# Two of seven Strassen products of the first FFN matmul by a second level of the scheme

## Chip, core and metric

The kernel runs on one core of a Trainium2 chip. The metric is the device time of one launch in microseconds. A launch is measured several times; the median counts. One further execution is recorded by the hardware profiler, and all profile rows come from that one.

The engines are called PE (TensorE, matmul; PEld are its weight loads), DVE (VectorE), ACT (ScalarE), POOL (GpSimd) and SP (SyncE, which only issues DMAs here). SBUF is the memory on the core, PSUM the memory into which PE writes (eight banks).

## What is computed

The input `x` is [64 batch, 64 rows, 1024]. Two layers follow one another, and the result is added to `x`:

```python
# 1. a state-space convolution along the last axis, masked by the length of the row
kernel = 2 * einsum('hn,hnl->hl', Cs, exp(dtA * arange(L))).real
y = irfft(rfft(u * mask, 2 * L) * rfft(kernel, 2 * L))[..., :L] + u * mask * D
y = y * mask
# 2. a gated low-rank FFN: 64 experts of rank 16, the best 16 per token
scores = xf @ Wr.T                                   # xf = y as [4096, 1024]
G = softmax over the top 16 of 64 scores, 0 elsewhere
h = einsum('nd,krd->nkr', xf, A)                     # first FFN matmul:  1024 x 1024 per token
out = einsum('nkr,kdr->nd', h * G[:, :, None], B)    # second FFN matmul: 1024 x 1024 per token
return x + 2.0 * out
```

All in fp32.

## The kernel before

**Groups.** The 64 rows are handled in 8 groups of 8 rows, so a group has 512 tokens. For each group g the kernel builds tables of the convolution (`tables`, DVE and ACT), makes states and their recurrence (`into_states`, L742 and `recur`, L786), the convolution itself on PE (`inside`, L828 and L836, and `across`, L851), brings the result from PSUM to SBUF with the mask (`evict`, L862, tile `y`), computes gates (`gates`, L941 to 986, and `spread_gates`, which sends them through HBM and back into tiles `gx` by POOL DMAs at L1007), and runs the first FFN matmul (`first`, `seven`). After the eighth group the second FFN matmul runs over pairs of groups (`second`, L1272); it is not touched except for the place from which it loads its rows.

**The first FFN matmul.** It is a matrix of 1024 x 1024 (left side, `wa`) times 1024 x 512 (right side, the group's `y`), by one level of Strassen's scheme in Winograd's form: both sides are cut into 2 x 2 blocks, the left factors are summed once at the start, the right factors for each group by DVE (`right_factors`), and seven products of 512 x 512 by 512 x 256 remain in place of eight. The left factors are `a11, a12, s4, a22, s1, s2, a21` for products 1 to 7; the right factors are `b11, b21, b22, t4, t1, t2, b12`.

`seven` goes over the seven products twice, for `j` = 0 and 2: each time for half of the 512 output rows. One product of one half is `product(n)`, L681 to 695: eight matmul calls (two row blocks `ii`, four steps `k` of the contraction) of 128 x 128 weights with 256 moving columns (L687). The results go to a PSUM bank of the pool `ps_f`, which has four. The order within a half and what happens to each product are:

- product 1 into bank `c11`, copied by ACT to `p1` (L702)
- product 6; DVE: `u2 = p1 - p6` (L709)
- product 2 added into `c11`
- product 7; DVE: `u3 = p7 + u2` (L716)
- product 5 into bank `c12`; DVE: `c22 = -u3 - c12` (L720, shown as L503 by the profile, the line of the helper)
- product 4; DVE: `u3 = p4 - u3` (L1050, shown as L492)
- product 3 added into `c12`; then `finish`

**`finish`** (L1027) multiplies the four blocks by their gates: block 11 by DVE straight out of PSUM (L1041), the others by POOL (L1034), into a tile `hg` with room for seven blocks. `hg` has one buffer. The first three blocks are stored to `hg_dram` by a POOL DMA; later `sums` makes the four sums that the second matmul wants as right factors (DVE, L492) and stores four more blocks. `sums` is called by `sum_factors` after the second step of the following half.

**Interleaving.** `seven` is a generator with seven steps per half, 14 per group. The main loop pulls steps between the parts of the next group's convolution: the last five steps of group g-1's products and the first five of group g lie between two convolutions' parts, four steps between `inside(0, 1)` and `inside(2, 3)`. Within the engines' queues the instructions are ordered by a planner when the program is built, from its own cost estimates; a few are pinned to the order of the source (`keep_in_program_order`) or behind another instruction (`issue_after`). So an instruction can stand earlier on its engine than in the source. Each engine then works through its queue in that order.

**Start.** Before the first group the left factors are loaded and summed: `s1` and `s2` through PE with an identity matrix, `a21` and `s4` by accumulating POOL DMAs (`third_sum`, L230, and `fourth_sum`, L236 and L239).

**SBUF.** It is full. 16384 bytes per partition are held back for the descriptors of POOL's DMAs.

Of the kernel before, what the change touches and what calls it, by code (L numbers as in the profile page):

```python
# [37 lines left out]
F32 = mybir.dt.float32  # L38
I32 = mybir.dt.int32
AF = mybir.ActivationFunctionType  # L40
ALU = mybir.AluOpType
# [3 lines left out]
P = 128  # L45
NB = 64
NH = 64
L = 1024
# [12 lines left out]
HT = TOK // NS2  # L61
KH = NBLK // 2
# [45 lines left out]
def body(ctx: ExitStack, tc, x, xo, lens, par, dvec, dgrp, at, bm, wt, cst, out):  # L108
    nc = tc.nc
# [6 lines left out]
    def pool(stack, name, bufs, side, **kw):  # L116
        return stack.enter_context(tc.tile_pool(name=name, bufs=bufs, side=side, **kw))
# [9 lines left out]
    fp = pool(ctx, "fp", 2, "left")  # L127
    gp = pool(left, "gp", 1, "left")
    tq = pool(left, "tq", 1, "left")
    ids = pool(ctx, "ids", 1, "right")  # L130
    const = pool(right, "const", 1, "right")
    xp = pool(right, "xp", 4, "right")
# [99 lines left out]
    def fourth_sum(s4, s2):  # L232

        for k in range(0, KH, 2):
            tc.keep_in_program_order(
                G.dma_start(s4[:, k : k + 2, :], at[:, KH + k : KH + k + 2, : L // 2]))  # L236
        for k in range(0, KH, 2):
            tc.keep_in_program_order(
                G.dma_start(s4[:, k : k + 2, :], s2[:, k : k + 2, :], accum_op=ALU.add))  # L239
# [247 lines left out]
    def new(name, w=NP, dtype=F32, keep=False):  # L487
        pool = const if keep else prep
        return pool.tile([P, w], dtype, tag=f"p_{name}", name=f"p_{name}")

    def tt(o, a, b, o_):
        V.tensor_tensor(out=o, in0=a, in1=b, op=o_)  # L492
        return o
# [8 lines left out]
    def stt(o, a, s, o1, b, o2):  # L502
        V.scalar_tensor_tensor(out=o, in0=a, scalar=s, in1=b, op0=o1, op1=o2)  # L503
        return o
# [169 lines left out]
        tt(t4, b21, t2, ALU.subtract)  # L674
        return b11, b21, b22, t4, t1, t2, b12

    def seven(fac, rf, j, name, finish, second_early=False):

        def product(n, bank=None, more=False):  # L681
            first = bank is None
            if first:
                bank = ps_f.tile([P, 2, HT], F32, tag="pf", name=f"{name}_{j}_{n}")
            for ii in range(2):
                for k in range(KH):
                    nc.tensor.matmul(  # L687
                        bank[:, ii, :],
                        lhsT=fac[n - 1][:, k, (j + ii) * P : (j + ii + 1) * P],
                        rhs=rf[n - 1][:, k, :],  # L690
                        start=(first and ii == 0 and k == 0),
                        stop=(ii == 1 and k == KH - 1 and not more),
                        skip_group_check=True,
                    )
            return bank

        def new(t, n=0):
            return fp.tile([P, 2, HT], F32, tag=t, name=f"{name}_{j}_{t}{n}")

        c11 = product(1, more=True)  # L700
        p1 = new("p", 1)
        marks["p1"] = nc.scalar.copy(p1, c11)  # L702
        yield
        if second_early:
            product(2, c11)
            yield
        p6 = product(6)
        u2 = new("u2")
        marks["u"] = V.tensor_tensor(out=u2, in0=p1, in1=p6, op=ALU.subtract)  # L709
        yield  # L710
        if not second_early:
            product(2, c11)
            yield
        p7 = product(7)
        u3 = new("u3")
        marks["u"] = V.tensor_tensor(out=u3, in0=p7, in1=u2, op=ALU.add)  # L716
        yield
        c12 = product(5, more=True)
        c22 = new("p", 5)
        stt(c22, u3, -1.0, ALU.mult, c12, ALU.subtract)  # L720
        yield
        p4 = product(4)
        yield
        product(3, c12)
        finish(j, c11, u2, u3, c12, p4, c22)
        yield


    begun = {}
# [39 lines left out]
    def conv(g, steps, out):  # L769
# [102 lines left out]
        if g == 0:  # L872
            step(1)
            into_states(0, 0, bt, states, more)
            into_states(0, 1, bt, states, more)
            step(3)
            masks()
            first_order.close()
            step(1)
            behind_landing(toep[0:1, HG - 1, 0:1])  # L880
            third_sum(wa_quarters[0])
            fourth_sum(wa[2], wa[5])
            prep_ctx.close()
            fourth.append(pool(right, "sp_more", 1, "right"))
        recur(0, 1)
# [128 lines left out]

    hg_dram = dram.tile([NG, P, 7, KH, HT], F32, tag="hg", name="hg_dram")

    def first(g, y, spread):

        v = y.rearrange("p k s h b -> p k s (h b)")

        rf = [v[:, :KH, 0, :], v[:, KH:, 0, :]]
        if g:
            rf[:] = right_factors(v, f"ty{g}_")

        def finish(j, c11, u2, u3, c12, p4, c22):  # L1027
            hg = hp.tile([P, 7, 2, HT], F32, tag="hg", name=f"hg_{g}_{j}")

            def gate(m, s):  # L1030
                return spread[m, j][:, :, s * HT : (s + 1) * HT]

            def gt_(o, a, b, op):
                G.tensor_tensor(out=o, in0=a, in1=b, op=op)  # L1034

            def store(a, b):
                nc.gpsimd.dma_start(hg_dram[g, :, a:b, j : j + 2, :], hg[:, a:b])  # L1037

            b11, b21, b22, t4, t1, t2, b12 = (hg[:, n] for n in range(7))
            def first_quarter():  # L1040
                i = V.tensor_tensor(out=b11, in0=c11, in1=gate(0, 0), op=ALU.mult)  # L1041
                if late_gates:
                    tc.keep_in_program_order(i)


            late_gates = g in (0, NG - 1)
            if not late_gates:
                first_quarter()
            gt_(b22, c22, gate(1, 1), ALU.mult)
            tt(u3, p4, u3, ALU.subtract)  # L1050
            gt_(b21, u3, gate(1, 0), ALU.mult)
            marks["u"] = V.tensor_tensor(out=u2, in0=c12, in1=u2, op=ALU.add)
            gt_(b12, u2, gate(0, 1), ALU.mult)
            if late_gates:
                first_quarter()
            store(0, 3)

            def sums():
                tt(t1, b11, b12, ALU.subtract)
                tt(b12, b22, b12, ALU.subtract)  # L1060
                tt(t2, b22, t1, ALU.add)
                tt(t4, b21, t2, ALU.subtract)
                store(3, 7)

            unsummed.append(sums)

        for j in range(0, KH, 2):
            for n, _ in enumerate(seven(wa, rf, j, f"h{g}", finish, g + j == 0)):
                if n == 1:
                    sum_factors()  # L1070
                yield
                if n == 1 and len(rf) == 2:

                    rf[:] = right_factors(v, f"ty{g}_")

    unsummed = []

    def sum_factors():
        while unsummed:
            unsummed.pop()()  # L1080
# [13 lines left out]
    def queued(o, i):  # L1094
        tc.keep_in_program_order(nc.sync.dma_start(o, i))

    def load_factor(sg, n, halves):
        for gg in range(2):
            queued(halves[gg], hg_dram[2 * sg + gg, :, n - 1])

    def second_sums(r, u1, u2, u4, pinned=False):

# [409 lines left out]
```

## Time and profile before

| | |
|---|---|
| median of 3 runs | 942.14 us (941.78 to 942.18) |
| the profiled execution | 941.79 us |
| its span, first to last instruction | 940.0 us |
| granted PE clock | 1.00 throughout |
| busy: PE, PEld, DVE, ACT, POOL | 929.5, 743.2, 741.0, 164.1, 337.0 us |
| matmul records at L687 (first FFN matmul) | 1792 |
| the first 55 us | tables and convolution of the first group, sums of the left side |
| 55 to 597 us | eight groups of products with the next group's convolution in between |
| 597 to 940 us | the second FFN matmul |

A row of a group reads: line, engine, operation, output and inputs by tile name, shape, count | busy time in us, mean ns of one | idle time of the engine just before, and what ended it. A row of the chain or the timeline reads: start in us, length in us, engine, line, operation, count. A matmul's own length is longer than the distance to the next one, as they are pipelined; the distance is what a stream costs.

### The profile page before, as it was taken

Reading aid. Unit: us, or ns where it says so; the run is one execution under the profiler, and the core shown is the slowest. Engines: PE = TensorE matmul, PEld = TensorE weight load, DVE = VectorE, ACT = ScalarE, POOL = GpSimd, SP = SyncE. Lnnn points to the kernel's source line nnn. Section 1 sums busy time; section 2 is a strip of 40 time slices with the busy share of each in tenths; the row PEclk is TensorE's granted clock in tenths of the full one; section 3 lists DMA queues with packets and bytes.
Section 4 is the critical chain, followed back from the end, with each engine's and each line's share of the span. In section 5 each row is a group of like instructions: output and inputs, shape, how many; then the busy total and the mean of one; then the engine's idle time right before and its main releaser. Section 6 shows DMA issues by size and latency. Waiting matters only on the chain.

```text
span 940.0 us, 14255 instructions
## 1 busy us (share of the span) xinstructions
PE 929.5 (99%) x5384; PEld 743.2 (79%) x5384; DVE 741.0 (79%) x1725; ACT 164.1 (17%) x314; POOL 337.0 (36%) x284
## 2 busy tenths in 40 slices
PE   7999999999999999999999999999999999999998
PEld 2576768688588588588588788888888888888887
DVE  8899798797996995995892497879856866785674
ACT  5343233411411411510300000000000000000000
POOL 0113213052052052052052032356746555764555
PEclk9999999999999999999999999999999999999999
DMA  8635335347454444444242463754672574358332
GB/s 291 186 87 168 107 110 156 108 126 189 125 144 154 124 138 159 125 128 169 90 131 101 152 246 124 255 203 140 212 275 79 191 270 155 110 205 307 95 123 101
DMA packets 72298, 149.47 MB, mean 159 GB/s; under 512 B 10054, under 2 KB 21030, under 8 KB 72230
## 3 DMA queue, kind: packets, MB, share of 16 engines
q1 hardware_dynamic: 52546, 99.65, 32.1%
q0 software_dynamic: 16864, 47.22, 16.0%
q10 hardware_dynamic: 2820, 1.70, 0.6%
q8 instruction: 42, 0.69, 0.3%
q14 instruction: 26, 0.21, 0.1%
HBM read 100.13 MB, written 47.33 MB: 157 GB/s over the span
## 4 chain that ended last, share of the span: by engine, by line
PE 93%; DVE 6%; issue 0%; DMA 0%; ACT 0%; DVEq 0%
PE h L687 39%; PE s L1272 35%; PE pu L742 5%; PE pc L851 4%; PE psh L947 3%; PE pc L828 3%; PE pc L836 1%; DVE bt L492 1%; DVE hg L492 1%; DVE f L492 1%; DVE f L503 0%; PE psc L959 0%; PE pb L440 0%; PE last L1272 0%; DMA par_sb<-in_par 0%
## 5 line engine op out<-in xcount | busy, mean ns | idle before, releaser
L786 DVE SCALAR_TENSOR_TENSOR s<-s,turn 128x64 f32<-128x64 f32 (+1 forms) x432 | 122.8, 330 | 2.8 <-ACT s L747 2.3
L687 PE MATMUL h<-y,waa 128*128 128x256 f32 x512 | 116.7, 380 | 0.0
L687 PE MATMUL h<-y,was 128*128 128x256 f32 x512 | 116.2, 379 | 0.0
L687 PE MATMUL h<-ty,was 128*128 128x256 f32 x512 | 116.0, 379 | 0.0
L687 PEld LDWEIGHTS h<-y,waa 128*128 128x128 f32 x512 | 96.3, 190 | 15.0 <-issue 1.9
L687 PEld LDWEIGHTS h<-ty,was 128*128 128x128 f32 x512 | 97.1, 190 | 13.9 <-issue 0.8
L687 PEld LDWEIGHTS h<-y,was 128*128 128x128 f32 x512 | 96.8, 190 | 13.7 <-DVE b L503 0.4
L1034 POOL TENSOR_TENSOR hg<-h_p,gx 128x512 f32<-128x512 f32 x16 | 35.6, 2223 | 141.6 <-DVE h_p L503 107.1
L1007 POOL DMA_DIRECT2D gx<-gt_dram x56 | 33.9, 618 | 145.1 <-DMA gt_dram<-gt 145.1
L1286 ACT COPY p<-s 128x512 f32<-128x512 f32 x28 | 16.4, 585 | 312.4 <-PE s L1272 312.4
L1034 POOL TENSOR_TENSOR hg<-h_u,gx 128x512 f32<-128x512 f32 x32 | 45.1, 1409 | 63.8 <-DVE h_u L492 36.6
L1131 POOL TENSOR_TENSOR o<-o,acc_a 128x512 f32<-128x512 f32 x32 | 47.6, 1506 | 41.4 <-ACT acc_a L1149 32.5
L687 PE MATMUL h<-ty,waa 128*128 128x256 f32 x256 | 58.4, 381 | 0.0
L687 PEld LDWEIGHTS h<-ty,waa 128*128 128x128 f32 x256 | 48.2, 190 | 8.3 <-DVE rsn L492 0.8
L742 PE MATMUL pu<-x,bt 128*64 128x448 f32 x256 | 53.0, 546 | 0.4
L862 DVE TENSOR_TENSOR y<-pc,mask 128x512 f32<-128x512 f32 x64 | 40.2, 680 | 16.4 <-PE pc L851 16.4
L1131 POOL TENSOR_TENSOR o<-o,b_room 128x512 f32<-128x512 f32 x32 | 49.1, 1555 | 9.8 <-DVE b_room L492 9.8
L492 DVE TENSOR_TENSOR o<-o,s 128x512 f32<-128x512 f32 x50 | 34.1, 681 | 23.0 <-PE s L1272 17.9
L1037 POOL DMA_DIRECT2D hg_dram<-hg x32 | 25.6, 800 | 67.4 <-DVE hg L492 46.6
L1131 POOL TENSOR_TENSOR o<-o,u 128x512 f32<-128x512 f32 x36 | 45.3, 1282 | 10.0 <-DVE u L492 9.7
L492 DVE TENSOR_TENSOR hg<-hg 128x512 f32<-128x512 f32 x64 | 42.4, 682 | 4.7 <-POOL hg L1034 4.3
L1272 PE MATMUL s<-qy,wbs 128*128 128x256 f32 x192 | 44.1, 379 | 0.0
(275 smaller groups left out, 1678.8 us busy)
## 6 DMA issues: line engine op xcount, KB each, us to landing
x<-in_x SPq DMA_DIRECT2D x32, 512.0 KB
hg_dram<-hg POOLq DMA_DIRECT2D x16, 1024.0 KB, 6.0
o<-in_xo SPq DMA_DIRECT2D x64, 256.0 KB
out<-o SPq DMA_DIRECT2D x63, 256.0 KB
gx<-gt_dram POOLq DMA_DIRECT2D x56, 256.0 KB, 4.8
qy<-hg_dram SPq DMA_DIRECT2D x28, 512.0 KB
r<-hg_dram SPq DMA_DIRECT2D x26, 512.0 KB
hg_dram<-hg POOLq DMA_DIRECT2D x16, 768.0 KB, 4.5
```

The lines of the kernel that those rows point to most:

```text
L492: V.tensor_tensor(out=o, in0=a, in1=b, op=o_)
L687: nc.tensor.matmul(bank[:, ii, :], lhsT=fac[n - 1][:, k, (j + ii) * P : (j + ii + 1) * P], rhs=rf[n - 1][:, k, :], start=(first and ii == ...
L742: nc.tensor.matmul(pu[hh * NS : (hh + 1) * NS, :], lhsT=bt[:, i, (1 - c) * P + hh * NS : (1 - c) * P + (hh + 1) * NS], rhs=xt[:, hh, : NCH ...
L786: return V.scalar_tensor_tensor(out=o, in0=a, scalar=scalar, in1=b, op0=op0, op1=op1)
L828: nc.tensor.matmul(pcs[hh][half_of(e, 1), chunks(e)], lhsT=toep[:, 2 * i + hh, HP:], rhs=xt[:, hh, chunks(e)], start=True, stop=False, ski ...
L851: m = nc.tensor.matmul(pcs[hh][half_of(e, late), into], lhsT=w[o : o + NS, c, i, seg : seg + HP], rhs=s[o : o + NS, c, of].rearrange("p k ...
L862: marks["y"] = V.tensor_tensor(out=y[:, :, i // 2, 2 * (i % 2) + hh, :], in0=pcs[hh].rearrange("p (k b) -> p k b", b=NB), in1=mask, op=ALU ...
L947: nc.tensor.matmul(phalf[o : o + NE, :], lhsT=wt_sb[:, d, :], rhs=yf[:, d, :], start=(d < 2), stop=(d >= NBLK - 2),)
L1007: i = queue.dma_start(gx[:, ii, :], gt_dram[g, c * n : (c + 1) * n, :].unsqueeze(1).to_broadcast([n, RANK, TOK]),)
L1034: G.tensor_tensor(out=o, in0=a, in1=b, op=op)
L1131: tc.keep_in_program_order(G.tensor_tensor(out=o, in0=a, in1=b, op=op_))
L1272: nc.tensor.matmul(bank[:, ii, :], lhsT=left_[i - 1][:, k, ii * P : (ii + 1) * P], rhs=right_[i - 1][:, k, :], start=(first and ii == rows ...
```

## The change

Three things change together.

1. Products 4 and 7 are computed by a second level of the same scheme, once for all four row blocks of the group rather than once for each half. Each becomes seven small products of 256 x 256 by 256 x 128 (`low`). A small product is four matmul calls with 128 moving columns. Their left factors are summed once at the start by POOL (`left_factors`, eight additions), the right ones per group by DVE (`low_rights`, four operations for each of the two). A new pool `lop` holds them. The results of both halves come out of one run in the first half; the second half's are kept (`u3_of`, `fourth_of`) and joined by POOL. A group still has 14 steps, nine in the first half and five in the second.
2. The sums of gated rows are written over the rows themselves: `hg` has room for four blocks in place of seven, still in one buffer. The rows are stored in three DMAs per half in place of two, in a new order of places (`SLOT`). `sum_factors` is called after the third step of a half in place of the second.
3. The room for the descriptors of POOL's DMAs is 2048 bytes per partition.

```diff
+    lop = pool(left, "lop", 1, "left")
...
+    def left_factors(n):
+        f, h = wa[n - 1], L // 4
+        e = lop.tile([P, 3, 2, h], F32, tag=f"e{n}", name=f"low_{n}")
+        a11, a12, a21, a22 = f[:, :2, :h], f[:, 2:, :h], f[:, :2, h:], f[:, 2:, h:]
+        s1, s2, s4 = e[:, 0], e[:, 1], e[:, 2]
+        for o, a, b in ((s1, a21, a22), (s2, a11, s1), (s4, a12, s2), (a21, a11, a21)):
+            tc.keep_in_program_order(G.tensor_tensor(out=o, in0=a, in1=b, op=ALU.add))
+        LOW[n] = a11, a12, s4, a22, s1, s2, a21
+
+    def low_rights(r, name):
+        e = lop.tile([P, 3, 2, H2], F32, tag="r", name=name)
+        r11, r12, r21, r22 = r[:, :2, :H2], r[:, :2, H2:], r[:, 2:, :H2], r[:, 2:, H2:]
+        u1, u2, u4 = (e[:, i] for i in range(3))
+        tt(u1, r11, r12, ALU.subtract)
+        tt(u2, r22, u1, ALU.add)
+        tt(r12, r22, r12, ALU.subtract)
+        tt(u4, r21, u2, ALU.subtract)
+        return r11, r21, r22, u4, u1, u2, r12
+
+    def low(n, rights, name, early, late):
+        def product(i, bank=None, more=False):
+            first = bank is None
+            if first:
+                bank = ps_f.tile([P, 2, HT], F32, tag="pf", name=f"{name}_{n}_{i}")
+            for ii in range(2):
+                for k in range(2):
+                    nc.tensor.matmul(
+                        bank[:, ii, :H2], lhsT=LOW[n][i - 1][:, k, ii * P : (ii + 1) * P],
+                        rhs=rights[i - 1][:, k, :], ...)
+            return bank
+        ...
+        c11 = product(1, more=True)
+        q1 = new("q1")
+        nc.scalar.copy(q1, c11[:, :, :H2])
+        q6 = product(6)
+        v2 = new("v2")
+        tt(v2, q1, q6[:, :, :H2], ALU.subtract)
+        early(v2)
+        q7 = product(7)
+        v3 = new("v3")
+        tt(v3, q7[:, :, :H2], v2, ALU.add)
+        product(2, c11)
+        late((0, 0), c11[:, :, :H2], None)
+        yield
+        c12 = product(5, more=True)
+        late((1, 1), c12[:, :, :H2], v3)
+        q4 = product(4)
+        late((1, 0), q4[:, :, :H2], v3)
+        product(3, c12)
+        late((0, 1), c12[:, :, :H2], None)
+        yield
...
+        for j in (0, 2):
...
+            if j:
+                u3 = u3_of[j]
+                G.tensor_tensor(out=u3, in0=u3, in1=u2, op=ALU.add)
...
+            if not j:
+                rights = low_rights(rf[6], f"{name}_r7")
...
+                for _ in low(7, rights, name, early, late):
+                    yield j
+            c12 = product(j, 5, more=True)
+            c22 = new(j, "p", 5)
+            stt(c22, u3, -1.0, ALU.mult, c12, ALU.subtract)
+            if j:
+                G.tensor_tensor(out=u3, in0=fourth_of[j], in1=u3, op=ALU.subtract)
+            yield j
+            if not j:
+                rights = low_rights(rf[3], f"{name}_r4")
+            product(j, 3, c12)
+            done = finish(j, c11, u2, c12, c22)
+            if not j:
+                yield j
                 ...
+                steps = low(4, rights, name, early, late)
+                next(steps)
+                yield j
+                next(steps)
+            done(u3)
+            yield j
...
             fourth_sum(wa[2], wa[5])
+            for n in (4, 7):
+                left_factors(n)
...
+    SLOT = {1: 0, 3: 1, 2: 2, 5: 3, 6: 4, 4: 5, 7: 6}
...
-            hg = hp.tile([P, 7, 2, HT], F32, tag="hg", name=f"hg_{g}_{j}")
+            hg = hp.tile([P, 4, 2, HT], F32, tag="hg", name=f"hg_{g}_{j}")
...
-            store(0, 3)
+            store(0, 2, 0)
             def sums():
-                tt(t1, b11, b12, ALU.subtract)
+                tt(b11, b11, b12, ALU.subtract)
                 tt(b12, b22, b12, ALU.subtract)
-                tt(t2, b22, t1, ALU.add)
-                tt(t4, b21, t2, ALU.subtract)
-                store(3, 7)
+                tt(b22, b22, b11, ALU.add)
+                tt(b21, b21, b22, ALU.subtract)
+                store(0, 4, 3)
...
+            def done(u3):
+                gt_(b21, u3, gate(1, 0), ALU.mult)
+                store(2, 3, 2)
+                unsummed.append(sums)
...
-                if n == 1:
+            if n == 2:
                 sum_factors()
...
-    nc = bacc.Bacc("TRN2", target_bir_lowering=False, num_devices=1)
+    nc = bacc.Bacc("TRN2", target_bir_lowering=False, num_devices=1, dynamic_dma_scratch_size=2048)
```

In `early` and `late` the quarters of the small scheme are put into `u3` of the first half and into the tile for the second half: `early` is one POOL operation of 256 columns, `late` one DVE operation of 256 columns.

## The prediction

> **What bounds the kernel now.** I read the page first (which engine is full), then the groups of instructions, the chain of work that ended last, the table by stage, and last the timeline around the products that the change touches.
>
> ```profile
> PE 929.5 (99%) x5384; PEld 743.2 (79%) x5384; DVE 741.0 (79%) x1725; ACT 164.1 (17%) x314; POOL 337.0 (36%) x284
> L687 PE MATMUL h<-y,waa 128*128 128x256 f32 x512 | 116.7, 380 | 0.0
> L1034 POOL TENSOR_TENSOR hg<-h_u,gx 128x512 f32<-128x512 f32 x32 | 45.1, 1409 | 63.8 <-DVE h_u L492 36.6 <-DVE h_u L1052 24.0 <-DMA o<-in_xo 3.2
> ```
>
> TensorE (PE) idles for 10.5 us of 940.0 in all. Whatever shortens its work shortens the kernel, as long as the other engines keep up. A busy PE is not yet PE at its peak rate, so the price of one matmul has to come from the distance of starts. One source matmul is two records, since 896 calls at L687 gave 1792 records. The chain, and the weight loads of one short window, give that distance:
>
> ```profile
> 253.41 34.53 PE h L687 x160
> 68.60 0.88 PE pb L440 x8
> 55.38 0.30 PEld L687 LDWEIGHTS h<-ty,was 128*128 128x128 f32 x2
> ```
>
> A record with 256 moving columns takes 34.53/160 = 0.216 us; a transpose with 128 moving columns takes 0.88/8 = 0.110 us. Two weight loads together last 0.30 us although one lasts 0.19, so the second begins 0.11 us after the first: loads can follow each other every 0.11 us.
>
> The table by stage (columns: stretch, length, then PE, weight loads, DVE, ACT, POOL busy) says how much room VectorE (DVE) has:
>
> ```profile
> 55.00:127.00 72.00, 72.00 (x485) 51.73 (x484) 64.78 (x196) 28.51 (x62) 15.80 (x18) 1.00 0.39 119
> 127.00:185.50 58.50, 58.50 (x414) 43.71 (x415) 47.68 (x163) 19.97 (x41) 10.55 (x13) 1.00 0.40 120
> 185.50:252.70 67.20, 67.08 (x452) 51.03 (x452) 61.14 (x171) 18.46 (x33) 19.41 (x18) 1.00 0.55 156
> 252.70:323.90 71.20, 71.07 (x472) 54.57 (x471) 61.09 (x168) 18.46 (x33) 18.59 (x18) 1.00 0.46 139
> 395.00:466.00 71.00, 71.00 (x472) 54.56 (x471) 57.38 (x158) 12.66 (x23) 18.60 (x18) 1.00 0.40 129
> 533.50:597.20 63.70, 63.70 (x298) 56.10 (x297) 55.80 (x99) 1.59 (x3) 16.52 (x12) 1.00 0.58 204
> 229.90:281.30 51.40, 51.28 (x311) 38.45 (x311) 51.22 (x149) 14.88 (x28) 14.64 (x15) 1.00 0.46 135
> ```
>
> A stretch between 55 and 597 us is about one group. PE has no room in any; DVE has 6 to 14 us (the stretch 323.9 to 395 reads like the one before it, 466 to 533.5 has 27 us). The last row is a part in which both are full for 51 us and PE still loses only 0.12: a full DVE alone does not stop PE.
>
> The DVE timeline shows two more things, a wait and a collision:
>
> ```profile
> 286.57 0.69 DVE L1041 TENSOR_TENSOR hg<-h,gx 128x512 f32<-128x512 f32 x1 [5.28 <-DMA hg_dram<-hg]
> 272.08 2.21 DVE L786 SCALAR_TENSOR_TENSOR s<-s,turn 128x128 f32<-128x128 f32 x1
> 274.21 0.34 DVE L786 SCALAR_TENSOR_TENSOR s_more<-s_more,turn 128x128 f32<-128x128 f32 x1
> ```
>
> The first gating of a half waits 5.28 us, at the head of DVE's queue, until the previous rows have been stored and their single buffer is free. And the same operation that takes 0.34 us takes 2.21 while GpSimd (POOL) runs a gating from 272.85 to 274.13.
>
> **PE.** The change takes away, in each of 8 groups, the products 4 and 7 of both halves: per product 2 halves × 8 calls × 2 records × 0.216 = 6.91 us. It adds seven small products of 4 calls with 128 columns: 56 records. No row shows such a record in a true product. The nearest is the transpose, 0.110 us; its weight load is shorter (140 ns against 190), but the pair of loads above allows 0.11 as well, and the row of 256 columns halved gives 0.108. I take 0.110: 6.16 us, 0.75 less. Sixteen times that is **−12.0 us**. From below: 0.108 gives −13.8. From above: if a load had to end before the next one began, 0.19 each, 10.6 us, +3.7 per product, +59 in all. The overlapping loads speak against that end, and break-even lies at 6.91/56 = 0.123 us.
>
> Here a page of the Trainium skill speaks against the change: "TensorE: Matmul & The Clock Gate", section "Back-to-back issue gap", says that in a stream of load and matmul pairs 128 columns cost about 81 ns where the formula for streaming alone gives 56. The transposes of this trace, which also load weights each time, show no such surcharge. If the page's ratio of 1.45 did apply to 0.110 us, an estimate from that page would be 0.16 us per record, 8.9 us per product and +32 us in all.
>
> **DVE.** A small product set has ten operations on 256 columns (four sums of the right side, two subtractions or additions on the way, four last ones); two such operations in a row start 0.33 us apart (257.95 and 258.28), so 20 cost 6.6 us per group. Four evictions of 512 columns go (four such in a row last 2.47 us, 0.60 apart): −2.4. That is +4.2. The four sums of gated rows stay four, now in place and one step later. On ACT two copies of 256 columns come on; at 17% busy they cost nothing.
>
> **POOL.** Per group two additions of 256 columns and two of 512 come on, at 1.41 us for 512: 4.2 us, and two more store issues at 0.8. It has 18.6 of 71 us busy, so they fit. But they collide with DVE. In the stretch from 252.7 to 466 the recurrence on the shape 128x128 takes 499 ns on average where the quiet tile `s_more` takes 323: 56 × 0.176 = 9.9 us against 18 gatings, 0.55 us each. Two full and two half additions: +1.6 on DVE. The least is 0 if they fall beside PSUM reads, the most 1.3 each, +3.9.
>
> So DVE gets +5.8 us per group (4.2 to 8.1) and PE −1.5. Setting the two beside each other, and allowing DVE 1 us of unavoidable idle (my choice; the full stretch shows 0.2 in 51, most stretches 5): 55 to 127 gives 70.6 against 70.5, 1.1 over; 185.5 to 252.7 gives 66.9 against 65.7, 2.2 over; 533.5 to 597.2 gives 61.6 against 62.2, 0.4 over; the others stay under by 2.5 or more. Sum **+3.7 us** of new waits of PE, with 0 and 23 as the ends (DVE +4.2 and no idle; +8.1 and 4 us of idle).
>
> **The eight sums of the left side** run once, on POOL, behind the DMAs of `third_sum` and `fourth_sum` (last one over at 50.52), the four for product 4 first. At 1.41 us they end at 61.8, at 2.22 (the slower gating row) at 68.3. Product 7 of group 0 begins at 58.1; its third small product, which needs the eighth sum, would start at 59.9. **+1.9 us**; the other end is +8.4, from which one product of 3.5 us can be put in between. Behind these sums stand the gate loads (67.62), which wait for the gates anyway.
>
> **At nothing:** the smaller descriptor scratch (its only users here, 32 stores and 56 gate loads, become 48 and 56, spread over 540 us; if issues did queue, POOL's own 50 idle us per group cover it), and the store order `SLOT`, since the second matmul reads the rows of groups 0 and 1 first, hundreds of us later.
>
> **Sum:** 941.79 (the profiled execution; span 940.0) − 12.0 + 3.7 + 1.9 = 935.4. The median of the runs lies 0.35 above that execution: 935.7 us.
>
> **Rivals.**
> 1. *All hidden.* DVE and POOL keep up, records at 0.108 to 0.110: 928 to 930. For it: the full DVE stretch without loss. Against it: stretches that come out over 100%. Chance 0.11.
> 2. *DVE is the bound.* The whole gain goes into its 5.8 us per group: 942 ± 1.9, which I call no change, as 0.2% is about what a measurement of this kernel can resolve. Chance 0.11.
> 3. *The buffer of gated rows turns into a PE wait; slower.* `hg` still has one buffer, and the sums that end in its store move one product later, next to the small products 7. Today's four waits (22.0 us in total in the chain of DVE's waits) cost PE nothing, because products of 3.46 us and four banks cover them. A small product lasts 0.88 us and each needs DVE; two free banks cover 1.8 us. Then each of the four waits costs 5.5 − 1.8 = 3.7, 14.8 together: 935.4 + 14.8 + 0.35 = 950.5. It decides from 1.6 us per wait on, where the forecast's 6.4 us are used up. In the second half it may strike too, as only two products (6.9 us) lie between the sums and the next gating, against 2.4 of sums, 0.8 of issue and 6.0 of landing. Against it: the order on DVE isn't that of the source, and gating can be put behind the small evictions. Chance 0.30.
> 4. *Loads bind:* above 0.123 us per record; at 0.19 about 1001. Chance 0.04. Late left sums and collisions at their upper ends without rival 3: about 946, chance 0.02.
>
> The forecast itself (931 to 940) has 0.42. Faster by over 0.2%: 0.42 + 0.11 = 0.53; same 0.11; slower 0.30 + 0.06 = 0.36. The range of 8 in 10 goes from 929 (all hidden) to 953 (rival 3 with a little of its second half). The faster cases alone would be 928 to 940.
>
> **What would show it.** Right: a small product's 8 records in 0.88 us; about 0.75 us less PE per product and group; DVE near 66 to 67 us in the middle stretches; PE idle in all 16 rather than 10.5 us, most of it near the left sums and between 55 and 67 us of a group. Rival 3 would show as waits of PE for DVE in small products while DVE stands at L1041's successor behind `hg_dram`. The step most likely wrong is DVE's +5.8 and where it falls. Distances above 0.123 between small records would make the whole prediction wrong.

## The result and the profile after

The changed kernel takes 1069.97 us (median of 4 runs, 1065.73 to 1072.81) against 941.99 of the kernel before beside it: 1.136 times as long, interval 1.132 to 1.139. Forecast were 935.7. The profiled execution of after took 1065.73, its span is 1063.9: 123.9 us more than before. The first stage ends at some 714 us instead of 597, the second is 7 us longer.

Of the page, the busy row and the granted clock (40 slices, tenths of full speed; before, all were 9):

```profile
PE 960.9 (90%) x5768; PEld 766.5 (72%) x5768; DVE 803.6 (76%) x1853; ACT 170.1 (16%) x330; POOL 400.1 (38%) x340
PEclk9989989999899899999989899898999999999999
```

PE (TensorE) got slower in two ways at once. It idles for 103.0 us (1063.9 − 960.9; before 10.5), although no other engine is full. And it is busy for longer than before with less work, because its clock was lowered at times (in 8 of the 40 slices it is below 0.9). Line numbers of after: the small products are L712, the ordinary ones L756, the first gating of a half L1163, POOL's gatings L1156, stores L1159, evictions of `y` L981, `pu` L861. L493 and L504 are the helpers `tt` and `stt`, told apart by tiles: `h_p<-h_u,h` is the operation `c22`, `h_u<-h_p,h` (L789) is `u2`, `h_v<-h_q,h` is a `v2` of the small scheme.

The table by stage (stretch, length, then PE, weight loads, DVE, ACT, POOL busy, granted clock, DMA):

```profile
55.00:145.00 90.00, 74.22 (x513) 54.15 (x513) 74.49 (x202) 27.03 (x59) 30.79 (x30) 0.91 0.30 96
215.00:298.00 83.00, 71.52 (x496) 53.62 (x495) 68.89 (x180) 17.52 (x33) 22.97 (x24) 0.94 0.43 123
384.00:470.00 86.00, 75.15 (x524) 57.44 (x524) 68.17 (x196) 19.28 (x35) 25.95 (x24) 0.98 0.38 116
645.00:714.00 69.00, 57.64 (x300) 50.85 (x299) 55.21 (x78) 1.92 (x4) 25.57 (x20) 0.93 0.40 133
```

Before, PE filled each such stretch (55 to 127 us was the first, 395 to 466 the fifth, 533.5 to 597.2 the last). Now it leaves 11 to 16 us of each of these open, and DVE (VectorE) 14 to 18. Two engines with room wait for each other. What for is in the waits, of DVE (two rows) and of PE (columns: us in total, times, longest):

```profile
DVE hg L493 <- DMA hg_dram<-hg: 46.6, 10, 7.6
DVE hg L1163 <- DMA hg_dram<-hg: 23.6, 5, 6.6
...
PE pu L861 <- DVE y L981: 20.4, 4, 5.5
PE h L712 <- DVE hg L1163: 17.7, 5, 5.2
PE h L756 <- DVE h_p L504: 13.0, 7, 5.0
PE h L712 <- DVE h_v L493: 10.5, 6, 6.4
PE h L712 <- DVE h_u L789: 6.1, 4, 3.0
```

The first row is new: the in-place sums wait for stores. The second is rival 3. The timeline shows how the first becomes PE's stop:

```profile
362.71 0.58 POOL L1159 DMA_DIRECT2D hg_dram<-hg  x1 [0.41 <-POOL hg L1156]
368.07 0.69 DVE L493 TENSOR_TENSOR hg<-hg 128x512 f32<-128x512 f32 x1 [3.07 <-DMA hg_dram<-hg]
368.68 1.28 DVE L981 TENSOR_TENSOR y<-pc,mask 128x512 f32<-128x512 f32 x2
369.42 5.12 PE L861 MATMUL pu<-x,bt 128*64 128x448 f32 x16 [5.33 <-DVE y L981]
```

At 362.71 POOL issues the store of block 21. The fourth sum is to be written over that block, so it waits until the store has landed. Behind it in DVE's queue stand the evictions of `y`, which have nothing to do with the block, and PE waits 5.33 us for the bank that they empty. Six stops of this kind, of 4.6 to 5.5 us, make 30.7 us: five at `pu` or at the transposes `pb`, the sixth at the start of the second matmul. Rival 3 looks like this:

```profile
328.49 2.05 PE L712 MATMUL h<-y,was 128*128 128x128 f32 x16 [1.04 <-DVE h_u L789]
333.02 0.69 DVE L1163 TENSOR_TENSOR hg<-h,gx 128x512 f32<-128x512 f32 x1 [4.59 <-DMA hg_dram<-hg]
333.63 0.41 DVE L493 TENSOR_TENSOR h_v<-h_q,h 128x256 f32<-128x256 f32 x1
333.77 1.16 PE L712 MATMUL h<-h_r,low 128*128 128x128 f32 x8 [3.23 <-DVE hg L1163]
```

Two small products run without a break (16 records in 2.05 us), then the four banks are used up. The gating reads its block straight out of a PSUM bank. PE goes on just after it ends (333.02 + 0.69 = 333.71), before the `v2` behind it is done (334.04): the next small product needed the bank that the gating held.

Two groups answer to those shown of before (columns: busy, mean ns of one | idle before, releaser):

```profile
L1156 POOL TENSOR_TENSOR hg<-h_u,gx 128x512 f32<-128x512 f32 x32 | 47.8, 1494 | 56.7 <-DVE h_u L493 29.5
...
L712 PE MATMUL h<-h_r,low 128*128 128x128 f32 x256 | 38.6, 297 | 29.0 <-DVE hg L1163 16.8
```

POOL's gating takes 1494 ns against 1409; the small records carry idle time (29.0 us in this row) that no row of L687 had before.

**A budget.** For every matmul record the distance from its start to the next start was taken from the trace, and set against the median distance of its shape. What is above the median goes to "idle" where the trace has PE idle ahead of the next record, to "half clock" where the granted clock was below 1, and to "hesitation" otherwise (a record lasts longer than the distance to the next one, so its tail can hide a short wait). "Stream" is the number of records times their median. Records on the edge between two classes can be put either way, which moves up to 4 us from one column to another. Differences to the kernel before, in us of the span, with four of the experiments below:

| kernel | span | stream | idle | half clock | hesitation |
|---|---|---|---|---|---|
| after | +123.9 | −9.3 | +95.7 | +25.4 | +12.0 |
| rows alone | +13.9 | −0.6 | +10.0 | +4.0 | +0.5 |
| product 7 alone | +45.0 | −5.3 | +36.8 | +9.7 | +3.7 |
| product 4 alone | +36.4 | −5.9 | +32.7 | +5.2 | +4.3 |
| cover alone | +14.8 | −1.1 | +12.3 | 0.0 | +3.6 |

The stream did what was forecast, nearly: −9.3 against −12.0. Hesitations alone use that up, before the first real stop.

### The profile page after: what moved, and what is told of

It is laid out like the page before. It is cut to its first block, busy times and chain, and to the rows that moved or that the text cites. A ratio compares the mean times of both kernels' runs of the same rounds, so it can differ in the third digit from the quotient of the medians.

```text
span 1063.9 us, 15314 instructions
## 1 busy us (share of the span) xinstructions
PE 960.9 (90%) x5768; PEld 766.5 (72%) x5768; DVE 803.6 (76%) x1853; ACT 170.1 (16%) x330; POOL 400.1 (38%) x340
## 5 line engine op out<-in xcount | busy, mean ns | idle before, releaser
L905 DVE SCALAR_TENSOR_TENSOR s<-s,turn 128x64 f32<-128x64 f32 (+1 forms) x432 | 117.1, 314 | 7.7 <-ACT s L866 6.8
L756 PE MATMUL h<-y,waa 128*128 128x256 f32 x512 | 118.2, 381 | 0.0
L756 PE MATMUL h<-ty,was 128*128 128x256 f32 x512 | 117.1, 381 | 0.6 <-DVE ty L493 0.6
L756 PEld LDWEIGHTS h<-ty,was 128*128 128x128 f32 x512 | 96.1, 190 | 16.6 <-issue 3.1
L756 PEld LDWEIGHTS h<-y,waa 128*128 128x128 f32 x512 | 96.3, 191 | 14.2 <-issue 1.2
L493 DVE TENSOR_TENSOR hg<-hg 128x512 f32<-128x512 f32 x64 | 45.6, 713 | 58.1 <-DMA hg_dram<-hg 46.6
L861 PE MATMUL pu<-x,bt 128*64 128x448 f32 x256 | 62.6, 628 | 20.4 <-DVE y L981 20.4
L756 PE MATMUL h<-y,was 128*128 128x256 f32 x256 | 61.5, 393 | 13.0 <-DVE h_p L504 13.0
L1159 POOL DMA_DIRECT2D hg_dram<-hg x48 | 34.0, 710 | 98.6 <-DVE hg L493 78.2
L1156 POOL TENSOR_TENSOR hg<-h_u,gx 128x512 f32<-128x512 f32 x32 | 47.8, 1494 | 56.7 <-DVE h_u L493 29.5
L1413 ACT COPY p<-s 128x512 f32<-128x512 f32 x28 | 16.4, 585 | 318.8 <-PE s L1399 318.8
L1156 POOL TENSOR_TENSOR hg<-h_p,gx 128x512 f32<-128x512 f32 x16 | 33.3, 2080 | 87.3 <-DVE h_p L504 83.2
L756 PEld LDWEIGHTS h<-y,was 128*128 128x128 f32 x256 | 48.3, 195 | 23.3 <-DVE h_p L504 16.2
L712 PE MATMUL h<-h_r,low 128*128 128x128 f32 x256 | 38.6, 297 | 29.0 <-DVE hg L1163 16.8
L861 PEld LDWEIGHTS pu<-x,bt 128*64 128x64 f32 x256 | 19.7, 157 | 59.8 <-DVE y L981 26.2
L792 POOL TENSOR_TENSOR h_u<-h_u,h_u 128x512 f32<-128x512 f32 x8 | 13.1, 1634 | 118.7 <-DVE h_u L789 104.4
L712 PEld LDWEIGHTS h<-h_r,low 128*128 128x128 f32 x256 | 35.0, 209 | 31.3 <-DVE hg L1163 17.5
L493 DVE TENSOR_TENSOR o<-o,s 128x512 f32<-128x512 f32 x50 | 34.1, 682 | 23.0 <-PE s L1399 17.3
```

What stands on the lines that cost most here:

```text
L712: nc.tensor.matmul(bank[:, ii, :H2], lhsT=LOW[n][i - 1][:, k, ii * P : (ii + 1) * P], rhs=rights[i - 1][:, k, :], start=(first and ii == 0 ...
L756: nc.tensor.matmul(bank[:, ii, :], lhsT=fac[n - 1][:, k, (j + ii) * P : (j + ii + 1) * P], rhs=rf[n - 1][:, k, :], start=(first and ii == ...
L792: G.tensor_tensor(out=u3, in0=u3, in1=u2, op=ALU.add)
L861: nc.tensor.matmul(pu[hh * NS : (hh + 1) * NS, :], lhsT=bt[:, i, (1 - c) * P + hh * NS : (1 - c) * P + (hh + 1) * NS], rhs=xt[:, hh, : NCH ...
L905: return V.scalar_tensor_tensor(out=o, in0=a, scalar=scalar, in1=b, op0=op0, op1=op1)
L1159: nc.gpsimd.dma_start(hg_dram[g, :, slot : slot + b - a, j : j + 2, :], hg[:, a:b])
```

## The experiments

"Theory T" says that the rows do it, because DVE stands behind stores; "S" blames the scratch; "U" the products. Later U is split in two. "V" (cover): the products that were taken out had given DVE the time to read a bank before PE needed it. "W": the work added on DVE and POOL is too much. Each paragraph names the measured median and the ratio to the kernel before, measured beside it (941.8 to 941.9 in all).

**1. The scratch alone.** `dynamic_dma_scratch_size=2048` in the kernel before.

> The kernel before with the third part of the change alone: 2048 bytes per partition for the descriptors of POOL's DMAs. Theory T (rows: the gated rows are summed where they are still being stored, so DVE stands behind stores, PE stops, and its clock falls): 942 us, no change, gate loads and stores land as before. Theory U (products: the small products of 0.88 us need DVE too often, whatever the rows do): 942 too. Theory S (scratch: a smaller room delays the issue of stores and gate loads): most of the 128 us are here, 1000 us or more, and the first gating's wait for hg_dram grows from 5.3 us.

941.88 us, ratio 1.000 (0.999 to 1.001). S is out. "At nothing" was right for the scratch.

**2. The rows alone.**

```diff
-            hg = hp.tile([P, 7, 2, HT], F32, tag="hg", name=f"hg_{g}_{j}")
+            hg = hp.tile([P, 4, 2, HT], F32, tag="hg", name=f"hg_{g}_{j}")
...
-                tt(t4, b21, t2, ALU.subtract)
-                store(3, 7)
+                tt(b21, b21, b22, ALU.subtract)
+                store(0, 4, 3)
...
-                if n == 1:
+                if n == 2:
```

> The kernel before with the second part alone: four blocks of gated rows summed in place, three stores, the new order of places, sums after the third step; all seven products stay ordinary. Theory T: 970 to 1010 us; DVE's sums wait for hg_dram some 40 us in all, just ahead of the evictions of y, PE then stops for 4 to 6 us and its granted clock falls to half behind the stops. Theory U: 942 to 948, since ordinary products of 3.46 us cover the waits. S: 942.

954.02 us, ratio 1.0126 (1.0102 to 1.0151). Less than T said, more than U. Of PE's waits, two stand out against the kernel before:

```profile
PE s L1274 <- DVE acc_a L503: 5.5, 1, 5.5
PE pb L440 <- DVE y L862: 3.2, 1, 3.2
```

DVE's sums wait for stores here too (15.4 us in all), but with ordinary products of 3.46 us around them nearly all of it is covered. One uncovered case is at the start of the second matmul, which also takes the last group's sums.

**3 and 4. One product alone**, the rows as before (seven blocks, two stores). For product 7:

```diff
-            for n in (4, 7):
+            for n in (7,):
                 left_factors(n)
...
+            p4 = product(j, 4)
+            tt(u3, p4, u3, ALU.subtract)
             yield j
             product(j, 3, c12)
```

and the mirror of it for product 4.

> The kernel after with product 7 alone at the second level (product 4 ordinary) and with the gated rows as before: seven blocks, two stores, sums after the second step. Theory T: 936 to 946 us (PE -6, four right sums and four last operations on DVE +2 per group, the left sums late by up to 4 us once), clock near 1.00. Theory U: 980 or more, half of the loss of both products and the waits for the first gating besides.

> The same with product 4 alone at the second level (product 7 ordinary), the gated rows as before. Theory T: 936 to 946 us, as for product 7; the first half's rows are finished as late as in the kernel after, so waits of the first gating for hg_dram may add up to 15 us. Theory U: 980 or more.

987.01 us (ratio 1.0492, 1.0461 to 1.0524) and 981.08 (1.0414, 1.0394 to 1.0434). T falls as the sole cause: with the rows left alone one product costs 45 us and the other 39. PE's largest waits in the DVE queue, first with product 7, then with product 4:

```profile
PE h L712 <- DVE hg L1144: 12.8, 5, 3.2
PE h L756 <- DVE h_p L504: 12.2, 4, 3.3
```

```profile
PE h L756 <- DVE h_p L504: 18.1, 9, 3.6
PE h L712 <- DVE h_f L504: 6.4, 6, 1.9
```

The wait `h_p` was in no step of the prediction. It is `c22`: DVE has to read product 5 out of its bank before product 3 is added into the same bank. Before, product 4 stood between the two and gave DVE 3.46 us. With product 4 at the second level, product 3 follows at once. The timeline with product 4 alone (DVE, and PE's last row):

```profile
433.58 0.27 DVE L887 SCALAR_TENSOR_TENSOR s_more<-s_more,turn 128x64 f32<-128x64 f32 x1
433.78 0.27 DVE L887 SCALAR_TENSOR_TENSOR s<-s,turn 128x64 f32<-128x64 f32 x1
433.97 0.27 DVE L887 SCALAR_TENSOR_TENSOR s_more<-s_more,turn 128x64 f32<-128x64 f32 x1
434.17 0.67 DVE L504 SCALAR_TENSOR_TENSOR h_p<-h_u,h 128x512 f32<-128x512 f32 x1
434.77 1.21 DVE L493 TENSOR_TENSOR ty<-y 128x1024 f32<-128x1024 f32 x1
434.89 0.91 PE L756 MATMUL h<-y,was 128*128 128x256 f32 x3 [1.37 <-DVE h_p L504]
```

DVE is not late with its work as a whole; recurrence steps that PE does not wait for here stand ahead of the one operation that it needs. That is theory V. With product 7 alone, product 4 still lies in between, and `c22` comes late all the same: DVE has stood at a `bt` behind a DMA, with table work and `c22` queued behind it:

```profile
DVE bt L493 <- DMA rf<-rows_of: 10.4, 4, 2.9
```

These four waits end some 6 us before PE's four stops for `c22` do. Without product 7 in the second half, PE gets there sooner.

**5 and 6. The waits for stores taken out of the kernel after**, one after the other, by order alone.

```diff
             if n == 2:
-                sum_factors()
+                with tc.issue_after(marks["y"].ins):
+                    sum_factors()
```

> The kernel after, with the four in-place sums held on DVE behind the evictions of y issued before them. Theory T (now for a part of the loss only: in the kernel after the sums stand on DVE behind a store, just ahead of the evictions of y, and PE stops six times for 4.6 to 5.5 us, 30.7 us, with half the clock afterwards): these stops go, some 30 us of idle and 10 to 15 of slow clock: 1020 to 1040 us. Theory V (cover: products 4 and 7 used to lie between a PSUM bank and its next use; without them PE waits at product 3 for DVE to read product 5's bank, and at the small products): 1050 or more, since the stops move to the next wait.

1043.55 us (ratio 1.1079, 1.1058 to 1.1100): 26.4 less than after. That is 3.5 above T's range and below V's. The five stops at `pu` and `pb` are gone but for 0.9 us; the sixth stayed:

```profile
PE s L1400 <- DVE acc_a L504: 5.8, 1, 5.8
```

The slow clock that T wanted to see go stayed too: PE is busy at half clock for 50.9 us, against 51.8 in after.

```diff
             if not late_gates:
-                first_quarter()
+                with tc.issue_after(marks["u"].ins):
+                    first_quarter()
```

> The same, and the first gating of a half held on DVE behind the last operation that feeds product 7's sum. Theory T (it waits for the single buffer of gated rows, 23.5 us of PE's stops in the kernel after): 20 to 35 us less than with the sums alone, 990 to 1015. Theory V: less than 10 us below the sums alone, since PE then stands at the next bank.

1014.74 us (ratio 1.0764, 1.0743 to 1.0785): 28.8 less again, as T said. The busy time at half clock falls to 37.6 us. T holds for this part: in the company of small products the waits behind stores, taken out by order alone, were worth 55 us; the rows alone cost 12. The wait of the first gating is in the kernel before as well, where it cost nothing.

**7 and 8. Product 2 put between products 5 and 3**, to give the cover back; the second run has the late sums too.

```diff
-            if not early_:
-                product(j, 2, c11)
-                yield j
...
             yield j
+            if not early_:
+                product(j, 2, c11)
+                yield j
             if not j:
                 rights = low_rights(rf[3], f"{name}_r4")
```

> The kernel after with product 2 moved between product 5 and product 3 (except in the first half of group 0): 3.46 us of matmuls lie again between product 5 and the product that adds into its bank, and c11 is complete only after the small products 7, so that its gating can't stand among them. Theory V: the 13 us of waits at product 3 and most of the 17 us of waits of small products for the first gating go, with 5 to 15 us of slow clock: 1025 to 1045 us. Theory T: 1045 to 1070, since the sums' waits are untouched.

> Both: product 2 between 5 and 3, and the sums behind the evictions of y. If V and T are parts of one sum: 975 to 1005 us, the two gains added; if each only uncovers the next wait of DVE: above 1015.

1057.18 us (ratio 1.1237) and 1048.52 (1.1155). The first lies in T's range and above V's, the second above 1015: each uncovers the next wait. In the first run the waits for `c22` and for the first gating shrink as V said (`c22` to 7.3 us, the gating out of the list), but another one grows in their place:

```profile
PE h L712 <- DVE h_u L789: 31.1, 8, 6.0
```

Product 2 had covered `u2` and the right sums ahead of the small products. One product of 3.46 us can't cover two places. In the second run the same wait is 44.2 us.

**9. The cover taken away alone**, in the kernel before.

```diff
+        p4 = product(4)
+        yield
         c12 = product(5, more=True)
         c22 = new("p", 5)
         stt(c22, u3, -1.0, ALU.mult, c12, ALU.subtract)
         yield
-        p4 = product(4)
-        yield
         product(3, c12)
```

> The kernel before (all products ordinary, rows as before) with product 4 moved ahead of product 5, so that product 3 follows product 5 at once and adds into a bank that DVE must first have read (c22): the cover that the change takes away, taken away alone, with no work added or removed. Theory V (cover: DVE's queue puts other work ahead of the operation PE needs, and the products 4 and 7 hid that): PE waits 1.4 to 3.5 us for c22 in most of the 16 halves, 960 to 990 us. Theory W (the losses that are left come from DVE's and POOL's added work alone): 942 to 945.

956.60 us (ratio 1.0157, 1.0140 to 1.0173). With not one operation added, the order costs 14.8 us:

```profile
PE h L687 <- DVE h_p L503: 5.5, 6, 1.1
PE pu L742 <- DVE y L862: 3.8, 3, 1.4
```

The direction is V's, the size smaller than its 960 to 990: PE waits for `c22` in 6 of the 16 halves, no stop of the two rows exceeds 1.4 us, and the clock stays at 1.00. Only 5.5 of the 14.8 us are waits at product 3 itself; the stops at `pu` and the hesitations (3.6 us in the budget) lie elsewhere.

**10. Product 2 moved in the second half only**, on top of experiment 6.

> The kernel after with sums and first gating held back (1014.7 us), and in the second half alone product 2 moved between 5 and 3, where no small product stands beside it. Theory V: the wait of product 3 for c22 (8 stops, 15.2 us) and some 5 us of slow clock go: 992 to 1002 us. Theory W: 1010 to 1018, the stop only moves to another product.

1027.50 us (ratio 1.0909), 12.8 more than without it. V's number failed, and W's too. The `c22` wait fell from 15.2 to 7.0 us, but `u2` rose from 3.2 to 18.2:

```profile
PE h L712 <- DVE h_u L789: 18.2, 7, 3.7
```

The planner that orders each engine's queue moved other DVE work when the products moved. In the first half of a later group, where nothing was edited, eleven recurrence steps now stand between the sums and `u2`, where there were none:

```profile
479.38 0.68 DVE L493 TENSOR_TENSOR hg<-hg 128x512 f32<-128x512 f32 x1
...
482.21 0.28 DVE L908 SCALAR_TENSOR_TENSOR s<-s,turn 128x64 f32<-128x64 f32 x1
482.40 0.68 DVE L789 TENSOR_TENSOR h_u<-h_p,h 128x512 f32<-128x512 f32 x1
```

An edit of the order isn't local.

**11. A lighter DVE**: experiment 6 without the recurrence (`for k in ():` in `recur`). DVE's busy time falls from 804.2 to 680.3 us.

> The kernel after with sums and first gating held back (1014.7 us), and without the recurrence of the states (its scalar_tensor_tensor operations, some 170 us of DVE's 804, are left out; nothing else is). If the stops that are left come from work that stands ahead on a full DVE (V and W both): 950 to 975 us, with PE idle below 35 us. If they are latencies that an empty DVE has too (operation after operation between banks of the small products): 1000 to 1015.

982.01 us (ratio 1.0436), between the two expectations: 32.7 less. This shows that a part of the stops comes from other work that stands ahead on DVE. It does not tell V from W, since both say that; no run adds the work and leaves the cover. The four middle groups, 250 to 580 us, have no PE stop over 1 us left. What stays is at the ends, as in experiment 6, whose timeline of DVE near the last group is:

```profile
611.57 3.09 DVE L243 TENSOR_TENSOR wbs<-wba,wbs 128x512 f32<-128x512 f32 x5
614.58 2.13 DVE L493 TENSOR_TENSOR hg<-hg 128x512 f32<-128x512 f32 x3
616.63 3.09 DVE L243 TENSOR_TENSOR wbs<-wba,wbs 128x512 f32<-128x512 f32 x5
619.64 0.41 DVE L493 TENSOR_TENSOR h_v<-h_q,h 128x256 f32<-128x256 f32 x1
...
620.11 1.22 PE L712 MATMUL h<-h_r,low 128*128 128x128 f32 x4 [6.35 <-DVE h_v L493]
```

Thirteen operations, ten for the second matmul's left side (`wbs`) and three sums, stand ahead of a `v2` of 0.41 us, and PE stops for 6.35.

**12. Product 7 alone, mended**: rows as before, the first gating held back, product 2 between 4 and 3 in the second half.

> Product 7 alone at the second level with the rows as before (987.0 us), the first gating held behind the operations of the small products, and in the second half product 2 put between 4 and 3. Theories T and V together: the waits for the first gating (12.8 us) and for c22 (12.2 us) go, with their slow clock (9 us): 945 to 958 us, PE's saving of 6 us still eaten by group 0 and by small stops. If every stop only uncovers the next: above 970.

969.22 us (ratio 1.0289, 1.0273 to 1.0306), 17.8 less than experiment 3 and still 27 above the kernel before. It lies between the two expectations, close to the second. The gating's wait went, `c22` kept 8.5 of its 12.2 us.

**13 to 15. The ends, and the base of the runs without the recurrence.** In the first, experiment 6 with the second level in groups 1 to 6 only (`0 < g < NG - 1`); in the second, the same without the recurrence; in the third, the kernel before without it.

> Sums and first gating held back (1014.7 us), and the second level only in groups 1 to 6; groups 0 and 7 compute products 4 and 7 in the ordinary way. If the loss that is left sits at the two ends, where the left sums come late and where the sums of the second matmul's left side stand on DVE ahead of the small products' operations: 975 to 992 us. If it is spread over all groups alike (a full DVE): 995 to 1003, that is a quarter of the 73 us less.

> The same without the recurrence of the states (some 170 us of DVE operations left out, nothing else). If PE's saving by the second level is real but half of what was forecast (0.42 us per small set against 0.75; 12 sets, 5 us), and all other losses are ends and a full DVE: 938 to 950 us. If the small products have a cost of their own that an empty DVE and quiet ends do not take away: above 960.

> The kernel before without the recurrence of the states (left out, nothing else), as the base of the runs that leave it out. PE bounds the kernel before by 99%, so 933 to 941 us, at most its 10 us of idle less; if DVE's fullness already cost something there that PE's busy time hides: below 930.

993.76 us (1.0558), 968.60 (1.0280) and 941.39 (0.9995, 0.9986 to 1.0005). Leaving the two end groups alone saves 21.0 us; a quarter of the 73 us would be 18. So the loss is spread over all groups, the ends only a little worse. The kernel before doesn't gain from a lighter DVE, the changed one gains 25.2. The second run missed 938 to 950 and came out on the other side, above 960. Its span is 24.1 us above the third's. By the same budget, against the kernel before (span +23.7): +18.6 idle, +3.6 half clock, and +1.4 for stream and hesitation together. The largest stop left is the place where the rows alone had stopped:

```profile
PE s L1410 <- DVE acc_a L504: 5.8, 1, 5.8
```

So even with these orders and with DVE at 70%, nothing is left of the gain: 12 of the 16 sets bring +1.4 us in PE's stream and hesitation, not minus. That counts all of PE's records. Those of the first FFN matmul alone (distance to the next start, at full clock and without idle time) come to 387 us against 390, some 3 us less; those of the convolution in between (L828, L836 and L851 of before) take some 3 us more. Why they do is not shown.

In one chain: order alone gave 26.4 and 28.8 us, a lighter DVE 32.7, ordinary products at the two ends 13.4 more, and 27.2 us over the kernel before without the recurrence stay. No version that was run with products at the second level comes below 941.99.

## Why the prediction was wrong, point by point

The step that failed is the term of +3.7 us for new waits of PE. It set DVE's busy time against the length of a stretch, and put the in-place sums at nothing. In its place PE idles 92.5 us longer (103.0 against 10.5) and works for 51.8 us at half clock, for which the sum had no term. The parts of the sum, one by one:

**What bounds the kernel: right.** PE did, with DVE not far behind. Experiment 15 shows the first half: 131 us less DVE work (610.3 against 741.0) leave the kernel before where it was (941.39 us against 941.83).

**PE, −12.0: the size held for the stream, and not for the net.** A small record follows the last one after 112 ns (median; 110 forecast), and weight loads don't bind: rival 4 is out. But the mean is 117.6 where clock and idle time don't disturb (784 of 896 records), since 53 come 15 to 115 ns late without recorded idle, 42 of them by 93 to 102. At 56 × 0.1176 = 6.59 us, against 32 × 0.2174 = 6.96 of an ordinary product at its own mean, a set saves 0.37, half of the 0.75. Of the late ones, 28 lie inside a set, 24 of them at the first record of a product, and 25 where other work follows. A chain of long products has fewer (28 in 1756 from 55 us on, in before). What makes them late is not shown.

**"Four sums stay four, now in place": the first half of the failed step.** It was put under no cost because the operations are the same. What they wait for is not: a sum written over a row waits for the store that reads the row (46.6 us of DVE's waits). Two questions weren't asked: what is queued behind the waiting operation, and who waits for that. The answer (evictions of `y`, then `pu`) was worth 26.4 us (experiment 5).

**Rival 3: the right mechanism, too low a price and a chance of 0.30.** Five waits stop PE for 17.7 us, as 14.8 said; taking them out gave 28.8 us (experiment 6), as half clock went with them.

**DVE, +3.7: the load was right, its effect wrong; the second half of the failed step.** DVE got 62.6 us more, 7.8 per group, inside the 4.2 to 8.1. But the sum compared busy time with the length of a stretch, as if DVE's queue could bring any operation when PE wants it. "A full DVE alone does not stop PE" was read from a stretch with ordinary products only, of 3.46 us each. The change takes products 4 and 7 out of the second half and puts sets of 0.9 us products into the first: it removes the cover that made the reading true. `c22`, `u2` and `v2` stop PE for 29.6 us (13.0 + 6.1 + 10.5). The prediction never asked what the removed products had been hiding. How much of this is lost cover and how much the added work itself stays open: experiment 9 shows the cover's direction at 14.8 us in the kernel before, and no run shows the added work alone. Two slips in the sum change nothing beside this: its upper end, worked out again from the same rows, is 29 us and not 23, and two of the stretches that "stay under by 2.5 or more" do so by 1.8 once the 1 us of idle is allowed for them too.

**The left sums, +1.9: their time about as forecast, their cost not shown.** The last left sum ends at 64.27 us, between the 61.8 and 68.3 of the forecast. The third small product, which needs it, starts only at 69.73, behind `u2` on DVE. The stop of 3.2 us ahead of the second one (64.70) is put down to POOL's sums in the row of the weight loads, and in the row of the matmuls to a right sum on DVE, which ends at 64.55. With it, three stops of group 0 between 60 and 70 us make 8.2, the other two for DVE's right sums and `u2`.

**No term at all: the clock.** The trace of before has 1.00 throughout, and nothing in it could show what a stop does. In after, PE is busy for 51.8 us at half clock, which is the +25.4 of the budget: a fifth of the loss. It is also a reason why the mended gating waits, 16.4 us in the kernel of experiment 5, gave 28.8: half clock went from 50.9 to 37.6 us.

## What to carry to other kernels

Before shortening or removing work on the full engine, list what that work covers: each operation on another engine that has its answer only because a product of known length stands in between. Where data is overwritten in place, add a wait for every reader still under way, DMAs above all, and ask what stands behind it in that engine's queue. A share of busy time says nothing on whether the one needed operation comes in time: count what stands ahead of it.

## What the runs showed of the hardware

**The clock falls after stops of 2 to 3 us.** In all traces together, after the first 12 us, there are 93 stops of PE of at least 1 us with no other of over 0.3 us within 12 us. Of the 24 below 1.8 us none is followed by half clock; of the 30 from 1.8 to 2.8 us, 9 are; of the 39 from 2.8 us on, all. The clock falls 2.0 to 5.3 us after the stop began, and stays at 0.5 for 3.4, 6.8 or 10.2 us. In 3.4 us at half clock PE loses 1.7 if it is busy throughout, so by this estimate a stop of 3 us costs nearer 5. The Trainium skill, "TensorE: Matmul & The Clock Gate", section "What's actually happening", speaks of a free-running window of some 3.4 us after which an idle PE is throttled to half. The steps of 3.4 us, and the undecided stops between 1.8 and 2.8, agree with a window that doesn't begin with the stop. The limit here is lower than one whole window of idle: 2.8 us were always enough.

**Weight loads keep up with 128 columns of fp32.** 731 of the 784 undisturbed small records of after are followed by the next record within 105 to 115 ns, with a load for each.
